# The ninth tap as plain fp32 products on four row groups

## The chip, the cores and the metric

The kernel runs on one core of one Trainium2 chip. The metric is the device time of one execution in microseconds, the median of several runs. The core has five engines with instruction queues of their own: TensorE (PE; its weight loads are shown apart, as PEld), VectorE (DVE), ScalarE (ACT), GpSimd (POOL) and SyncE (SP), which here only issues transfers.

## The reference

The input x has 4 images of 16 channels, 256 x 256, fp32. There are two layers, each a residual block on a group norm (`_gn`, 8 groups). The change touches only the first:

```python
def _L0_conv_ref(x, conv_w, conv_b):
    out = conv_general_dilated(x, conv_w, (1, 1), 'SAME') + conv_b    # 16 -> 16*25 channels, 3 x 3
    logits = out.reshape(N, C, K * K, H, W)                           # K = 5
    weights = softmax(logits, axis=2)                                 # over the 25 places
    return einsum('ncuij,ncuij->ncij', _unfold(x), weights)           # weighted mean of a 5 x 5 window

x = x + _L0_conv_ref(_gn(x), conv_w, conv_b)
x = x + _L1_conv_ref(_gn(x), ...)                                     # splines and SiLU, then 3 x 3
```

With h = `_gn(x)`, every pixel and channel gets 25 logits from a 3 x 3 convolution of h. A softmax over them weighs the 5 x 5 window of h around the pixel.

## The kernel before

**Where the data lie.** h is written to device memory in two layouts. `hs` holds rows of h, by strips of 32 columns, for the windows (`u`). `hst` holds h transposed, one column of 128 rows after another, for the convolution. A third array `hsl` holds h transposed in two parts: `hi`, h rounded to the type fp32r, and `lo`, the rest h - `hi`, also in fp32r.

**Getting h.** `normalize` (L276 on) is a generator; each `yield` is a place where the main loop goes on with its own work. `rows` has ScalarE scale x into `hsp` (L346) and `ht` (L359). `columns` transposes four blocks of `ht` on TensorE into `tp` (L384), copies `tp` to `tt` (fp32) and to `hi` (L375 to L381, `hi` always on ScalarE), and has VectorE subtract to `lo` (L396). Small copies carry the border rows of each half (L329, L330, L377 to L381, L405). `put_columns` then issues three writes, `tt` to `hst` and `hi` and `lo` to `hsl` (L319). Half of image 0 is normalized before layer 0 begins (`part=0`), among the statistics of x; the other half and images 1 to 3 go on inside layer 0, one image ahead. So while the last image is worked on, nothing of this remains.

**Layer 0.** The loop runs over 64 strips (4 images, 2 halves of 128 rows, 8 strips of 32 columns). The 128 rows of a half are the partitions of the result. A strip has eight steps of four columns (`JG = 4`). One column is a convolution of 128 pixels: 9 taps x 16 channels = 144 rows of weights, and a bias. 128 of them fit into one product: `am` holds eight taps of h (8 x 16 partitions) for eight columns, and `wm` their weights, both fp32 (L878). The ninth tap and the bias go into a second product (L882) with 97 rows in fp32r: `an` holds `hi` and `lo` twice each and a row pair of ones, `wn` the weights, rounded and rest, so that the products of the halves add up to about fp32. Each fp32 product stands in the profile as two weight loads and two passes, each fp32r product as one of each.

A column's 400 logits lie in one bank of `lg`, two columns to a tile, three such tiles in turn. ScalarE takes two columns at a time out of `lg` with an exponential into `e` (L901), GpSimd multiplies `e` with the window `u` (L906), and VectorE sums both over the 25 places into `nd` (L738), one step later. After eight steps VectorE divides (L758 to L760) with a reciprocal from ScalarE (L752, L754), GpSimd subtracts from x (L766), and every fourth strip ScalarE takes statistics for the next layer's norm (L786).

`e` has four buffers, `am` and `an` three each (`NIM = 3`), `u` two. All loads stand in SyncE's queue: `am` (three, L686) and `an` (two, L696) for eight columns, asked for two blocks ahead, and `u` (five, L710) for a strip, asked for at the middle of the strip before. The writes of `normalize` are in the same queue. Instructions are in the program's order on each engine (`in_order`).

**Layer 1** follows on the same engines. What matters of it here is that its products (L1082, L1092) use 32 columns of weights, in four column groups, and that L1092 changes between 64 and 128 rows.

**Before layer 0**, `prepare0` builds `wm` and `wn`, and a bound on the logits from the weights (`wps`, `times`) and from x decides whether the softmax needs a shift. It doesn't with these inputs (`shift` is false).

Of the kernel before, what the change touches and what calls it, by code (L numbers as in the profile page):

```python
# [12 lines left out]
F32 = mybir.dt.float32  # L13
F32R = mybir.dt.float32r
# [21 lines left out]
def conv_preact_kernel(  # L36
# [16 lines left out]
    P = 128  # L53
# [34 lines left out]
    hsl = [[dram.tile([C, 2, CT], F32, name=f"hsl{b}_{h}") for h in range(NH)] for b in range(B)]  # L88

# [27 lines left out]
    KT = 6 * C + 1  # L117
    wn = const.tile([KT, K, C, K], F32R, name="wn")

# [103 lines left out]
    NIM = 3  # L223

    def norm_tiles(prep):


        xps = [prep.tile([P, QC, W + 2 * PAD], F32, name=f"xp{h}", bufs=1) for h in range(NH)]
        tts, his, los = [
            [prep.tile([P, NH, QG, RP], d, name=f"{v}{n}", bufs=1) for n in range(2)]  # L230
            for v, d in (("tt", F32), ("hi", F32R), ("lo", F32R))
        ]
# [3 lines left out]
        for t in (*tts, *his, *los):  # L236
            t = t if t.dtype == F32 else t.bitcast(F32)
            nc.gpsimd.memset(t[:, 0, :, 0:1], 0.0)
            nc.gpsimd.memset(t[:, NH - 1, :, RP - 1 :], 0.0)
        return prep, xps, tts, his, los  # L240
# [7 lines left out]
    def zeros(b, queue):  # L248

        for e in (0, HP - PAD):  # L250
            for r in range(PAD):
                yield partial(
                    queue.dma_start,
                    hs[b][:, e + r].rearrange("s c w -> c s w"),
                    zero[0:C, 0 : NST * SP].rearrange("c (s w) -> c s w", s=NST),
                )
        for h in range(NH):
            for w in (0, (W + 1) * RP):
                yield partial(queue.dma_start, hst[b][h][:, w : w + RP], zero[0:C, 0:RP])
                yield partial(  # L260
                    queue.dma_start,
                    hsl[b][h][:, :, w : w + RP].rearrange("c t r -> (c t) r"), zero[:, 0:RP],
                )
# [4 lines left out]
    kept = [  # L268
        const.tile([P, C // QC * NQ, QG, 1], d, name=f"kept{i}") for i, d in enumerate((F32, F32R, F32R))
    ]  # L270

    def normalize(b, ptr, tiles, held=None, copier=None, part=None, dense=False):
# [5 lines left out]
        prep, xps, tts, his, los = tiles  # L278
# [32 lines left out]
        def put_columns(q, n):  # L311
            g0 = n * QG
            for h in parts:

                for to, ti, t in ((hst, 0, tts[n]), (hsl, 0, his[n]), (hsl, 1, los[n])):
                    d = to[b][h]
                    m = 2 if to is hsl else 1
                    t = t if t.dtype == F32 else t.bitcast(F32)
                    nc.sync.dma_start(  # L319
                        bass.AP(  # L320
                            tensor=d.tensor,
                            offset=d.offset + q * QC * m * CT + ti * CT + (1 + g0) * RP,
                            ap=[[QW * RP, W // QW], [m * CT, QC], [1, QG * RP]],
                        ),
                        t[:, h].rearrange("p g r -> p (g r)"),
                    )

        def border(t):
            nc.scalar.copy(t[:, 1, :, 0:1], t[:, 0, :, P : P + 1])  # L329
            nc.scalar.copy(t[:, 0, :, RP - 1 :], t[:, 1, :, 1:2])  # L330
# [37 lines left out]
        def columns(q, n, h):  # L368
# [3 lines left out]
            def copy(t, to, keep):  # L372

                if h in parts:
                    to(t[:, h, :, 1 : 1 + P], tp)  # L375
                if part == 1:
                    to(t[:, 1, :, 0:1], keep[:, q * NQ + n])  # L377
                elif h == 1:
                    to(t[:, 0, :, RP - 1 :], tp[:, :, 0:1])
                else:  # L380
                    to(t[:, 1, :, 0:1] if part is None else keep[:, q * NQ + n], tp[:, :, P - 1 :])  # L381

# [6 lines left out]
            copy(tts[n], copier, kept[0])  # L389
            copy(his[n], nc.scalar.copy, kept[1])  # L390
            if not dense:
                yield

            v = slice(1, 1 + P) if h in parts else slice(RP - 1, RP)
            to = h if h in parts else 0
            nc.vector.tensor_sub(  # L396
                los[n][:, to, :, v], tp[:, :, 0 : v.stop - v.start],
                his[n][:, to, :, v].bitcast(F32),
            )
            if part == 0 and h == 0:  # L400
                moves.append((1, partial(
                    nc.scalar.copy, kept[2][:, q * NQ + n], los[n][:, 0, :, P : P + 1]
                )))
            if part == 1:
                nc.scalar.copy(los[n][:, 1, :, 0:1], kept[2][:, q * NQ + n])  # L405
            if h == NH - 1:
                if part is None:
                    moves.append((5, partial(border, los[n])))
                moves.append((9 if part is None else 4, partial(put_columns, q, n)))
# [32 lines left out]
    with tc.tile_pool(name="prep0", bufs=2) as prep, tc.tile_pool(  # L442
# [29 lines left out]
        wnr = pre.tile([KT, NL], F32, name="wnr")  # L472
        nc.vector.memset(wnr, 0.0)
        v = conv_wt[2, 2 * C : 3 * C]
        for r in (0, 2 * C):
            nc.sync.dma_start(
                wnr[r : r + 2 * C, :],
                bass.AP(tensor=v.tensor, offset=v.offset, ap=[v.ap[0], [0, 2], [1, NL]]),
            )
        for r in (4 * C, 6 * C):  # L480
            nc.sync.dma_start(wnr[r : r + 1, :], conv_b)
# [24 lines left out]
        def prepare0():  # L506
# [3 lines left out]

            wp = pre.tile([KT, K, C, K], F32, name="wp")
            for m in range(K):
                nc.gpsimd.tensor_copy(wm[:, m], places(wr)[:, m])
                nc.gpsimd.tensor_copy(wp[:, m], places(wnr)[:, m])
            whi = pre.tile([KT, K, C, K], F32R, name="whi")
            nc.scalar.copy(whi, wp)
            nc.vector.tensor_sub(wn, wp, whi.bitcast(F32))
            nc.scalar.copy(wn[0 : 2 * C], wp[0 : 2 * C])
            nc.scalar.copy(wn[4 * C : 4 * C + 1], wp[4 * C : 4 * C + 1])

            aw = pre.tile([P, 2, NL], F32, name="aw")
            nc.scalar.activation(aw[:, 0], wr, AF.Square)
            nc.scalar.activation(aw[0:KT, 1], wnr, AF.Square)
            times = pre.tile([KT, 1], F32, name="times")
            nc.vector.memset(times, 0.0)
            nc.vector.memset(times[0 : 4 * C], 0.25)
            nc.vector.memset(times[4 * C : 4 * C + 1], 1.0)  # L530
            nc.tensor.matmul(wps, lhsT=onec, rhs=aw[:, 0], start=True, stop=False)
            nc.tensor.matmul(wps, lhsT=times, rhs=aw[0:KT, 1], start=False, stop=True)
# [125 lines left out]
    def layer0(shift):  # L658
# [4 lines left out]
        with tc.tile_pool(name=f"prep{arm}", bufs=2) as prep, tc.tile_pool(  # L663
# [6 lines left out]
            ans = [imp.tile([KT, CI * RP], F32R, name=f"an{n}{arm}", bufs=1) for n in range(NIM)]  # L670
            for t in ans:

                nc.vector.memset(t.bitcast(F32)[4 * C : KT], 1.0)
# [4 lines left out]
            def load_im(n):  # L678
# [14 lines left out]
                an = ans[n % NIM]  # L693
                d = hsl[b][hf]
                for r in (0, 2 * C):
# [7 lines left out]
                return am, an  # L703

            def load_u(n):
                b, hf, s = strips[n]
                u = l0.tile([P, K, C, SP], F32, name=f"u_{n}{arm}", tag="u")
# [125 lines left out]
            ims.append(load_im(1))  # L833
            nxc, xc = load_xc(0), None
            ahead = iter(())
            for n, (b, hf, s) in enumerate(strips):
# [23 lines left out]
                for j in range(0, SW, JG):  # L860
                    if j % CI == 0:
                        k = n * nci + j // CI
                        if k + 2 < len(strips) * nci:
                            ims.append(load_im(k + 2))
                        am, an = ims.pop(0)
# [7 lines left out]
                    e = l0.tile([P, 2, JG, K, C, K], F32, name=f"e_{n}_{j}{arm}", tag="e", bufs=LAG + 3)  # L873
                    for j1 in range(0, JG, 2):
                        lg = plog.tile([P, 2, 512], F32, name=f"lg_{n}_{j}_{j1}{arm}", tag="lg")
                        for i in range(2):
                            o = (j + j1 + i) % CI * RP
                            nc.tensor.matmul(  # L878
                                lg[:, i, :NL], lhsT=am[:, o : o + P],
                                rhs=wm.rearrange("p m c d -> p (m c d)"), start=True, stop=False,  # L880
                            )
                            nc.tensor.matmul(  # L882
                                lg[:, i, :NL], lhsT=an[:, o : o + P],
                                rhs=wn.rearrange("p m c d -> p (m c d)"), start=False, stop=True,
                            )
# [321 lines left out]
```

## Time and profile before

| | us |
|---|---|
| median of 3 runs | 3048.94 (3048.42 to 3060.75) |
| span of the profiled execution | 3050.8 |
| first to last L878 product of layer 0 (start) | 113.8 to 2022.8 |
| busy in that stretch of 1909 us: PE, DVE, ACT, POOL | 1823, 1882, 1206, 1857 |
| share of the DMA engines in that stretch | 0.80 |
| DMA bytes over the span | 628 MB |

Busy times count when an instruction of the engine was under way. The ends of matmuls are modelled, and consecutive ones overlap in their pipeline, so what TensorE needs is read from the distance of the starts and not from busy time. "Idle before" is how long an engine stood still ahead of the instructions of a group, and "<-" what released it.

### The profile page before, as it was taken

To read this page: it belongs to the slowest core of one execution; us is meant where nothing else is said; L and a number is where in the kernel's file an instruction comes from. 1 tells how busy PE (TensorE), PEld (TensorE's weight loads), DVE (VectorE), ACT (ScalarE), POOL (GpSimd) and SP (SyncE) were. 2 spreads that over 40 slices of the span, in tenths; PEclk is the share of its full clock that TensorE was granted. 3 is DMA by queue.
4 is the path that set the end of the run, shared out by engine and by line. 5 is a ranking of instruction groups with operands and counts; after the bars stand their busy time and mean duration, and the time that the engine had idled before them with its cause. 6 is when DMAs were issued, how large, how long until landed. Compare 5 with 4: busy or idle time off the path is not lost.

```text
span 3050.8 us, 39867 instructions
## 1 busy us (share of the span) xinstructions
PE 2804.2 (92%) x14280; PEld 1447.6 (47%) x14280; DVE 2954.8 (97%) x1587; ACT 2252.1 (74%) x2619; POOL 1948.5 (64%) x744
## 2 busy tenths in 40 slices
PE   4699999999989999999999999958999999999998
PEld 3465656656656666666666556632222222222222
DVE  7599999999999999999999999999999999999997
ACT  6566776576765666766645646559999999999996
POOL 4399999999999999999999999980100100000000
PEclk7799999999999999999999999979999999999999
DMA  8988988878978778878857667659999999999993
GB/s 274 254 232 223 261 238 238 230 196 247 244 207 229 201 207 226 241 209 228 234 152 194 179 165 191 162 128 208 201 192 195 195 195 190 199 195 199 192 199 86
DMA packets 353042, 628.40 MB, mean 206 GB/s; under 512 B 41394, under 2 KB 218788, under 8 KB 336964
## 3 DMA queue, kind: packets, MB, share of 16 engines
q1 hardware_dynamic: 320132, 607.39, 81.0%
q10 hardware_dynamic: 30960, 15.73, 1.7%
q8 instruction: 117, 1.92, 0.3%
q0 software_dynamic: 1744, 2.64, 0.3%
q14 instruction: 89, 0.73, 0.1%
HBM read 516.05 MB, written 104.24 MB: 203 GB/s over the span
## 4 chain that ended last, share of the span: by engine, by line
DVE 68%; issue 12%; PE 9%; DMA 5%; ACT 3%; POOL 2%; SPq 1%; DVEq 0%; POOLq 0%; ACTq 0%
DVE nd L738 43%; PE lg L878 6%; DVE ta L169 4%; DVE ta L168 4%; DVE tb L169 4%; DVE tb L168 4%; DVE tb L159 2%; PE lg L882 2%; DVE yo L1065 1%; POOL e L906 1%; DVE r L759 1%; DMA an<-hsl 1%; DVE nd L758 1%; DVE nd L760 1%; DVE lo L396 1%
## 5 line engine op out<-in xcount | busy, mean ns | idle before, releaser
L906 POOL TENSOR_TENSOR e<-e,u 128x1600 f32<-128x1600 f32 x512 | 1788.5, 3543 | 56.4 <-ACT e L901 49.0
L878 PE MATMUL lg<-wm,am 128*128 128x400 f32 x4096 | 1735.7, 505 | 80.3 <-ACT e L901 49.1
L738 DVE TENSOR_REDUCE nd<-e 128x128 f32<-128x3200 f32 x512 | 1749.2, 3478 | 24.3 <-POOL e L906 24.3
L882 PE MATMUL lg<-wn,an 97*128 97x400 f32 x2048 | 1344.3, 656 | 12.8 <-DMA an<-hsl 12.7
L901 ACT ACTIVATE e<-lg 128x800 f32<-128x800 f32 x1024 | 820.0, 837 | 682.8 <-DVE nd L738 440.7
L878 PEld LDWEIGHTS lg<-wm,am 128*128 128x128 f32 x4096 | 759.9, 192 | 400.1 <-ACT e L901 104.5
L1082 PE MATMUL yp<-ring,wt 128*32 128x512 f32 x6144 | 745.3, 597 | 86.6 <-DVE ring L170 62.6
L882 PEld LDWEIGHTS lg<-wn,an 97*128 97x128 f32 x2048 | 388.1, 190 | 330.7 <-issue 21.7
L1082 PEld LDWEIGHTS yp<-ring,wt 128*32 128x32 f32 x6144 | 202.2, 109 | 621.6 <-issue 433.1
L999 POOL MEMSET sl<- 16x256 f32 x6 | 1.8, 306 | 402.9 <-PE yp L1092 396.8
L169 DVE TENSOR_TENSOR ta<-ta,ta 128x2048 f32<-128x2048 f32 (+1 forms) x64 | 147.4, 2303 | 3.0 <-ACT ta L167 2.9
L170 DVE SCALAR_TENSOR_TENSOR ring<-ta,ta 128x2048 f32<-128x2048 f32 (+1 forms) x64 | 147.8, 2310 | 2.5
L786 ACT ACTIVATE z<-xc,nrm 128x256 f32<-128x256 f32 x240 | 144.2, 601 | 6.4 <-POOL xc L766 2.4
L170 DVE SCALAR_TENSOR_TENSOR ring<-tb,tb 128x2048 f32<-128x2048 f32 x64 | 145.6, 2275 | 2.5
L169 DVE TENSOR_TENSOR tb<-tb,tb 128x2048 f32<-128x2048 f32 x64 | 145.2, 2269 | 0.0
L1092 PE MATMUL yp<-sl,ws 64*32 64x512 f32 (+1 forms) x1032 | 131.2, 602 | 0.0
L999 POOL MEMSET slc<- 16x256 f32 x2 | 0.6, 309 | 203.1 <-PE yp L1092 203.0
L167 ACT ACTIVATE ta<-ta 128x2048 f32<-128x2048 f32 (+1 forms) x64 | 123.4, 1928 | 2.0
L194 POOL TENSOR_TENSOR d<-d,nrz 128x8 f32<-128x8 f32 x4 | 2.7, 680 | 189.9 <-DVE d L192 189.9
L167 ACT ACTIVATE tb<-tb 128x2048 f32<-128x2048 f32 x64 | 120.6, 1884 | 0.0
L1018 ACT ACTIVATE sl<-sl,q 64x2048 f32<-64x2048 f32 x43 | 90.0, 2094 | 1.2
L766 POOL TENSOR_TENSOR xc<-xc,nd 128x512 f32<-128x512 f32 x64 | 82.8, 1293 | 8.3 <-DVE nd L760 8.3
(200 smaller groups left out, 2108.8 us busy)
## 6 DMA issues: line engine op xcount, KB each, us to landing
am<-hst SPq DMA_DIRECT2D x512, 194.6 KB
u<-hs SPq DMA_DIRECT2D x320, 288.0 KB
an<-hsl SPq DMA_DIRECT2D x512, 129.8 KB
xta<-x1s SPq DMA_DIRECT2D x40, 1024.0 KB
xtb<-x1s SPq DMA_DIRECT2D x40, 1024.0 KB
xtc<-x1s SPq DMA_DIRECT2D x40, 1024.0 KB
am<-hst SPq DMA_DIRECT2D x256, 129.8 KB
sl<-x1s SPq DMA_DIRECT2D x166, 128.0 KB
```

The source lines that it names most:

```text
L167: nc.scalar.activation(s1, r1, AF.Square, scale=2.0)
L168: nc.vector.scalar_tensor_tensor(s2, t, 2.0, s2, ALU.subtract, ALU.mult)
L169: nc.vector.tensor_mul(s1, s1, r1)
L170: nc.vector.scalar_tensor_tensor(f, s2, 0.0, s1, ALU.min, ALU.subtract if given else ALU.add)
L738: nc.vector.tensor_reduce(nd[:, :, :, j : j + JG].rearrange("p t c j -> p t j c"), e.rearrange("p t j m c d -> p t j c m d"), AX.XY, ALU.add,)
L786: nc.scalar.activation(z, v, f, scale=nrm[b][:, 0, g : g + 1], bias=nrm[b][:, 1, g : g + 1], accum_out=st1[b][:, t, g, columns_of(n) : col ...
L878: nc.tensor.matmul(lg[:, i, :NL], lhsT=am[:, o : o + P], rhs=wm.rearrange("p m c d -> p (m c d)"), start=True, stop=False,)
L882: nc.tensor.matmul(lg[:, i, :NL], lhsT=an[:, o : o + P], rhs=wn.rearrange("p m c d -> p (m c d)"), start=False, stop=True,)
L901: nc.scalar.activation(ev, lg[:, :, :NL], AF.Exp)
L906: nc.gpsimd.tensor_tensor(e[:, 1].rearrange("p j m c d -> p j (m c) d"), e[:, 0].rearrange("p j m c d -> p j (m c) d"), uv, ALU.mult,)
L1082: nc.tensor.matmul(yp[t * M : (t + 1) * M], lhsT=wt[:, d, e].rearrange("p r o -> p (r o)"), rhs=ring[:, r0 + t * RT + d : r0 + t * RT + d ...
L1092: nc.tensor.matmul(yp[t * M : (t + 1) * M], lhsT=ws[v, e].rearrange("p r o -> p (r o)"), rhs=sl[n % 3][v, t : t + NT + 1 : NT, e : e + W], ...
```

## The change

The ninth tap and the bias become one plain fp32 product of 17 rows (16 channels and a row of ones). Four columns are put on the partitions 0, 32, 64 and 96 of one tile, `wn` is there four times, and the four products of a step stand behind its eight-tap products, each on 32 rows of the array. `hi`, `lo`, `hsl` and everything that made and moved them go. The new tile `ans` holds a whole strip: row group r has the columns r, r+4, r+8 and so on, loaded by four transfers from `hst`, inside `load_u`. `am` gets a fourth buffer and is asked for three blocks ahead, `u` gets a third.

```diff
-    KT = 6 * C + 1
-    wn = const.tile([KT, K, C, K], F32R, name="wn")
+    KT = C + 1
+    RG = 32
+    wn = const.tile([P, K, C, K], F32, name="wn")
...
-    NIM = 3
+    NIM = 4
...
-            copy(tts[n], copier, kept[0])
-            copy(his[n], nc.scalar.copy, kept[1])
+            t, keep = tts[n], kept[:, q * NQ + n]
+            if h in parts:
+                copier(t[:, h, :, 1 : 1 + P], tp)
...
-            nc.vector.tensor_sub(
-                los[n][:, to, :, v], tp[:, :, 0 : v.stop - v.start],
-                his[n][:, to, :, v].bitcast(F32),
-            )
...
-            ans = [imp.tile([KT, CI * RP], F32R, name=f"an{n}{arm}", bufs=1) for n in range(NIM)]
+            ans = [imp.tile([P, SW // JG, P], F32, name=f"an{n}{arm}", bufs=1) for n in range(3)]
...
-                an = ans[n % NIM]
-                d = hsl[b][hf]
-                for r in (0, 2 * C):
+                return am
+
+            def load_u(n):
+                b, hf, s = strips[n]
+                d = hst[b][hf]
+                for r in range(JG):
                     nc.sync.dma_start(
-                        an.bitcast(F32)[r : r + 2 * C, 0:run],
+                        ans[n % 3][r * RG : r * RG + C],
                         bass.AP(
-                            tensor=d.tensor, offset=d.offset + (j0 + 2) * RP + 2,
-                            ap=[[2 * CT, C], [CT, 2], [1, run]],
+                            tensor=d.tensor, offset=d.offset + (s * SW + r + 2) * RP + 2,
+                            ap=[[CT, C], [JG * RP, SW // JG], [1, P]],
                         ),
                     )
-                u = l0.tile([P, K, C, SP], F32, name=f"u_{n}{arm}", tag="u")
+                u = l0.tile([P, K, C, SP], F32, name=f"u_{n}{arm}", tag="u", bufs=3)
...
-            ims.append(load_im(1))
+            ims += [load_im(1), load_im(2)]
...
-                        if k + 2 < len(strips) * nci:
-                            ims.append(load_im(k + 2))
+                        if k + 3 < len(strips) * nci:
+                            ims.append(load_im(k + 3))
...
+                    lgs = [
+                        plog.tile([P, 2, 512], F32, name=f"lg_{n}_{j}_{j1}{arm}", tag="lg")
+                        for j1 in range(0, JG, 2)
+                    ]
+                    for i in range(JG):
+                        o = (j + i) % CI * RP
+                        nc.tensor.matmul(
+                            lgs[i // 2][:, i % 2, :NL], lhsT=am[:, o : o + P],
+                            rhs=wm.rearrange("p m c d -> p (m c d)"), start=True, stop=False,
+                        )
+                    for i in range(JG):
+                        k = slice(i * RG, i * RG + KT)
+                        nc.tensor.matmul(
+                            lgs[i // 2][:, i % 2, :NL], lhsT=ans[n % 3][k, j // JG],
+                            rhs=wn[k].rearrange("p m c d -> p (m c d)"), start=False, stop=True,
+                        )
                     for j1 in range(0, JG, 2):
-                        lg = plog.tile([P, 2, 512], F32, name=f"lg_{n}_{j}_{j1}{arm}", tag="lg")
-                        for i in range(2):
-                            o = (j + j1 + i) % CI * RP
-                            nc.tensor.matmul(
-                                lg[:, i, :NL], lhsT=am[:, o : o + P],
-                                rhs=wm.rearrange("p m c d -> p (m c d)"), start=True, stop=False,
-                            )
-                            nc.tensor.matmul(
-                                lg[:, i, :NL], lhsT=an[:, o : o + P],
-                                rhs=wn.rearrange("p m c d -> p (m c d)"), start=False, stop=True,
-                            )
+                        lg = lgs[j1 // 2]
```

In `put_columns` one write of `tt` is left of three. `prepare0` places `wn` directly and needs no rounded copy and no `times`.

More of the change, by code (lines that the diff above doesn't have):

```diff
@@ L2 @@
 from functools import partial
-from itertools import chain
 from itertools import chain
@@ L86, in conv_preact_kernel @@
     hst = [[dram.tile([C, CT], F32, name=f"hst{b}_{h}") for h in range(NH)] for b in range(B)]
-    hsl = [[dram.tile([C, 2, CT], F32, name=f"hsl{b}_{h}") for h in range(NH)] for b in range(B)]
     CP = H * W + 1024
@@ L222, in conv_preact_kernel @@
     nrz = [const.tile([P, 2, G], F32, name=f"nrz{b}") for b in range(B)]
-    NIM = 3
+    NIM = 4
     def norm_tiles(prep):
         xps = [prep.tile([P, QC, W + 2 * PAD], F32, name=f"xp{h}", bufs=1) for h in range(NH)]
[L229 to L232, printed above, removed]
+        tts = [prep.tile([P, NH, QG, RP], F32, name=f"tt{n}", bufs=1) for n in range(2)]
         for t in xps:
@@ L235, in norm_tiles @@
             nc.gpsimd.memset(t[:, :, PAD + W :], 0.0)
-        for t in (*tts, *his, *los):
-            t = t if t.dtype == F32 else t.bitcast(F32)
+        for t in tts:
             nc.gpsimd.memset(t[:, 0, :, 0:1], 0.0)
             nc.gpsimd.memset(t[:, NH - 1, :, RP - 1 :], 0.0)
-        return prep, xps, tts, his, los
+        return prep, xps, tts
     zero = const.tile([PAD * C, max(RP, NST * SP)], F32, name="zero")
@@ L259, in zeros @@
                 yield partial(queue.dma_start, hst[b][h][:, w : w + RP], zero[0:C, 0:RP])
-                yield partial(
-                    queue.dma_start,
-                    hsl[b][h][:, :, w : w + RP].rearrange("c t r -> (c t) r"), zero[:, 0:RP],
-                )
     NQ = QW // QG
-    kept = [
-        const.tile([P, C // QC * NQ, QG, 1], d, name=f"kept{i}") for i, d in enumerate((F32, F32R, F32R))
-    ]
+    kept = const.tile([P, C // QC * NQ, QG, 1], F32, name="kept")
     def normalize(b, ptr, tiles, held=None, copier=None, part=None, dense=False):
-        prep, xps, tts, his, los = tiles
+        prep, xps, tts = tiles
         copier = copier or nc.scalar.copy
@@ L313, in put_columns @@
             for h in parts:
[L315 to L325, printed above, removed]
-                    )
-        def border(t):
-            nc.scalar.copy(t[:, 1, :, 0:1], t[:, 0, :, P : P + 1])
-            nc.scalar.copy(t[:, 0, :, RP - 1 :], t[:, 1, :, 1:2])
+                d = hst[b][h]
+                nc.sync.dma_start(
+                    bass.AP(
+                        tensor=d.tensor, offset=d.offset + q * QC * CT + (1 + g0) * RP,
+                        ap=[[QW * RP, W // QW], [CT, QC], [1, QG * RP]],
+                    ),
+                    tts[n][:, h].rearrange("p g r -> p (g r)"),
+                )
         hts = {}
@@ L370, in columns @@
             tp = ptr.tile([P, QG, P], F32, name=f"tp{b}_{q}_{n}_{h}", tag="tp")
[L372 to L381, printed above, removed]
             for k in range(QG):
@@ L388, in columns @@
                 yield
-            copy(tts[n], copier, kept[0])
-            copy(his[n], nc.scalar.copy, kept[1])
+            t, keep = tts[n], kept[:, q * NQ + n]
+            if h in parts:
+                copier(t[:, h, :, 1 : 1 + P], tp)
+            if part == 1:
+                copier(t[:, 1, :, 0:1], keep)
+            elif h == 1:
+                copier(t[:, 0, :, RP - 1 :], tp[:, :, 0:1])
+            else:
+                copier(t[:, 1, :, 0:1] if part is None else keep, tp[:, :, P - 1 :])
             if not dense:
                 yield
-            v = slice(1, 1 + P) if h in parts else slice(RP - 1, RP)
-            to = h if h in parts else 0
-            nc.vector.tensor_sub(
-                los[n][:, to, :, v], tp[:, :, 0 : v.stop - v.start],
-                his[n][:, to, :, v].bitcast(F32),
-            )
[L400 to L405, printed above, removed]
             if h == NH - 1:
-                if part is None:
-                    moves.append((5, partial(border, los[n])))
-                moves.append((9 if part is None else 4, partial(put_columns, q, n)))
+                moves.append((5 if part is None else 4, partial(put_columns, q, n)))
             yield
@@ L471, in conv_preact_kernel @@
             )
-        wnr = pre.tile([KT, NL], F32, name="wnr")
+        wnr = pre.tile([P, NL], F32, name="wnr")
         nc.vector.memset(wnr, 0.0)
-        v = conv_wt[2, 2 * C : 3 * C]
-        for r in (0, 2 * C):
[L476 to L481, printed above, removed]
+        for r in range(0, P, RG):
+            nc.sync.dma_start(wnr[r : r + C, :], conv_wt[2, 2 * C : 3 * C])
+            nc.sync.dma_start(wnr[r + C : r + KT, :], conv_b)
         nm = 3 * C
@@ L509, in places @@
                 return t.rearrange("p (c m d) -> p m c d", c=C, m=K)
-            wp = pre.tile([KT, K, C, K], F32, name="wp")
             for m in range(K):
                 nc.gpsimd.tensor_copy(wm[:, m], places(wr)[:, m])
[L514 to L519, printed above, removed]
+                nc.gpsimd.tensor_copy(wn[:, m], places(wnr)[:, m])
             aw = pre.tile([P, 2, NL], F32, name="aw")
             nc.scalar.activation(aw[:, 0], wr, AF.Square)
[L526 to L530, printed above, removed]
+            nc.scalar.activation(aw[0:KT, 1], wnr[0:KT], AF.Square)
             nc.tensor.matmul(wps, lhsT=onec, rhs=aw[:, 0], start=True, stop=False)
-            nc.tensor.matmul(wps, lhsT=times, rhs=aw[0:KT, 1], start=False, stop=True)
+            nc.tensor.matmul(wps, lhsT=onec[0:KT], rhs=aw[0:KT, 1], start=False, stop=True)
         def prepare1():
@@ L669, in layer0 @@
         ) as plog, tc.tile_pool(name=f"prc{arm}", bufs=1, space=PSUM) as prc:
-            ans = [imp.tile([KT, CI * RP], F32R, name=f"an{n}{arm}", bufs=1) for n in range(NIM)]
+            ans = [imp.tile([P, SW // JG, P], F32, name=f"an{n}{arm}", bufs=1) for n in range(3)]
             for t in ans:
-                nc.vector.memset(t.bitcast(F32)[4 * C : KT], 1.0)
+                nc.vector.memset(t, 1.0)
             tiles = norm_tiles(prep)
@@ L692, in load_im @@
                     )
-                an = ans[n % NIM]
-                d = hsl[b][hf]
-                for r in (0, 2 * C):
+                return am
[3 more added lines that the diff above has]
+                for r in range(JG):
                     nc.sync.dma_start(
-                        an.bitcast(F32)[r : r + 2 * C, 0:run],
+                        ans[n % 3][r * RG : r * RG + C],
                         bass.AP(
-                            tensor=d.tensor, offset=d.offset + (j0 + 2) * RP + 2,
-                            ap=[[2 * CT, C], [CT, 2], [1, run]],
-                        ),
-                    )
-                return am, an
-            def load_u(n):
-                b, hf, s = strips[n]
-                u = l0.tile([P, K, C, SP], F32, name=f"u_{n}{arm}", tag="u")
+                            tensor=d.tensor, offset=d.offset + (s * SW + r + 2) * RP + 2,
+                            ap=[[CT, C], [JG * RP, SW // JG], [1, P]],
+                        ),
+                    )
+                u = l0.tile([P, K, C, SP], F32, name=f"u_{n}{arm}", tag="u", bufs=3)
                 for m in range(K):
@@ L862, in layer0 @@
                         k = n * nci + j // CI
-                        if k + 2 < len(strips) * nci:
-                            ims.append(load_im(k + 2))
-                        am, an = ims.pop(0)
+                        if k + 3 < len(strips) * nci:
+                            ims.append(load_im(k + 3))
+                        am = ims.pop(0)
                     if j == SW // 2:
@@ L873, in layer0 @@
                     e = l0.tile([P, 2, JG, K, C, K], F32, name=f"e_{n}_{j}{arm}", tag="e", bufs=LAG + 3)
[L874 to L885 removed]
+                    lgs = [
[13 more added lines that the diff above has]
+                            rhs=wn[k].rearrange("p m c d -> p (m c d)"), start=False, stop=True,
+                        )
+                    for j1 in range(0, JG, 2):
+                        lg = lgs[j1 // 2]
                         ev = e[:, 0, j1 : j1 + 2].rearrange("p j m c d -> p j (m c d)")
```

## The prediction

> **What bounds the kernel now.** I first read the granted clock (0.975 over the whole span, 0.99 between 113.8 and 2022.8 us, so the clock is no issue), then the busy times in stretches, then the groups of layer 0, then single stretches of the timeline. Layer 1 is not touched by the change; layer 0 runs from the first `lg` product at 113.8 us to the last one at 2022.8 us. The groups of the window from 113 to 2040 us (busy time, mean ns of one, idle time before them):
>
> ```profile
> L906 POOL TENSOR_TENSOR e<-e,u 128x1600 f32<-128x1600 f32 x512 | 1788.5, 3543 | 56.4 <-ACT e L901 49.0 <-DMA u<-hs 3.9 <-DMA an<-hsl 3.4
> L738 DVE TENSOR_REDUCE nd<-e 128x128 f32<-128x3200 f32 x512 | 1749.2, 3478 | 24.3 <-POOL e L906 24.3
> L901 ACT ACTIVATE e<-lg 128x800 f32<-128x800 f32 x1024 | 820.0, 837 | 682.8 <-DVE nd L738 440.7 <-PE lg L882 220.0 <-DMA u<-hs 8.2
> L396 DVE TENSOR_TENSOR lo<-tp,hi 128x512 fp32r<-128x512 f32 x56 | 38.1, 681 | 0.0
> L384 PE MATMUL tp<-ident,ht 128*128 128x128 f32 x224 | 34.1, 274 | 0.0
> ```
>
> The reader sees three engines close together. A strip of 32 columns is eight steps of four columns. VectorE paces it, as the last image shows:
>
> ```profile
> 1500.58 27.23 DVE L738 TENSOR_REDUCE nd<-e 128x128 f32<-128x3200 f32 x8
> 1527.73 0.68 DVE L758 TENSOR_TENSOR nd<-nd,r 128x512 f32<-128x512 f32 x1
> 1528.44 0.70 DVE L759 SCALAR_TENSOR_TENSOR r<-nd,r 128x512 f32<-128x512 f32 x1
> 1529.17 0.69 DVE L760 TENSOR_TENSOR nd<-nd,r 128x512 f32<-128x512 f32 x1
> 1529.78 27.23 DVE L738 TENSOR_REDUCE nd<-e 128x128 f32<-128x3200 f32 x8
> ```
>
> From 1500.58 to 1529.78 is 29.2 us with no gap. In images 0 to 2 each `lo` of L396 lengthens a strip by 0.6 us, to 29.8 or 30.4. GpSimd needs 8 x 3.49 (1788.5 / 512) + 1.29 (L766) = 29.2 us per strip as well: no edit of the change touches that, so **29.2 us per strip is a floor**. TensorE starts a column every 0.855 us (0.338 from the first pass of L878 to its second, 0.026 to the record of L882, 0.49 to the next column), 3.42 us per step, 27.4 us per strip, plus 0.6 us per group of four transposes. Its reserve is only 29.2 - 27.4 = 1.8 us per strip, **0.22 us per step**.
>
> **The products, part by part.** Today a column has two passes of `wm` and one L882 pass. The stream of one fp32 pass of 400 columns is about 0.335 us; the L882 pass takes 0.855 - 2 x 0.34 = 0.175 us, 0.70 us for four columns. New: 8 `wm` passes of 0.34 = 2.72 us, then four columns on four row groups, two passes each, 0.335 us per pass. If the four groups run abreast that is 2 x 0.335 + 0.02 = 0.69 us: the same as today. The trace has no row groups, but column groups of fp32 in layer 1, at 0.112 us for a 512-column instruction (10.51 / 94) against a stream of 0.335 x 512/400 = 0.43 us, so 3.8 abreast:
>
> ```profile
> 3015.34 10.51 PE yp L1082 x94
> ...
> 3025.84 2.98 PE yp L1092 x24
> ```
>
> What is new is that TensorE changes its shape twice a step, from whole array to quarter rows and back. Two rows price it. The first is L207, a 16-row product between two columns of layer 0, where nothing else changes:
>
> ```profile
> 1778.38 0.83 PE L878 MATMUL lg<-wm,am 128*128 128x400 f32 x2
> 1778.74 0.65 PE L882 MATMUL lg<-wn,an 97*128 97x400 f32 x1
> 1779.32 0.38 PE L207 MATMUL ps<-q,sel 16*128 16x2 f32 x2
> 1779.63 0.94 PE L878 MATMUL lg<-wm,am 128*128 128x400 f32 x2
> ```
>
> The next column would have come at 1778.38 + 0.855 = 1779.23; L207 starts only at 1779.32, 0.09 after the stream before it has ended, and its weights are loaded then and not ahead. Afterwards the `wm` pair takes 0.94 instead of 0.83 to 0.84: its weight load of 128 columns stands exposed for 0.10. So one change costs 0.09 + 0.10, about 0.20 us. The second row is L1092, where 64-row and 128-row products of 32 columns alternate (weight loads, eight in each shape):
>
> ```profile
> 2068.28 0.15 PEld L1092 LDWEIGHTS yp<-sl,ws 64*32 64x32 f32 x8 [0.84 <-issue]
> 2069.27 0.16 PEld L1092 LDWEIGHTS yp<-sl,ws 128*32 128x32 f32 x8 [0.84 <-issue]
> 2070.27 0.15 PEld L1092 LDWEIGHTS yp<-sl,ws 64*32 64x32 f32 x8 [0.84 <-issue]
> ```
>
> Two rounds of 0.43 are 0.86, the spacing is 1.00: 0.14 us per change. I take 0.20, from L207, because it has the 128 columns of weights and lies in this very stage; 0.14 stays as the lower bound, and for the upper see the third case below. A step is then 2.72 + 0.69 + 2 x 0.20 = **3.81 us** (3.69 with 0.14), against 3.65 for VectorE and GpSimd. TensorE becomes the bound.
>
> A rule of the Trainium skill speaks against the change: "TensorEngine Tiling (Array Packing)", Key Properties, says that a change of tiling mode drains the array, which the gap before L207 agrees with; it gives no time. The same skill, "TensorE: Matmul & The Clock Gate", Measured speedup vs the span model, has 3.07 times for four row tiles; by it the four columns would take 4 x 0.67 / 3.07 = 0.87 us, an estimate, and a step 3.99 us.
>
> **The layer.** 512 x 3.81 = 1951, plus 56 transpose groups x 0.6 = 34, plus waits. Of today's 1909 us, 512 x 3.42 + 34 = 1785 are work and 124 are waits. Most of these are VectorE's pace handed back through `e` and `lg` (PE and PEld waiting for ACT e L901, 49 and 104 us overlapping) and vanish when TensorE is slower; I keep 15, what its waits for `am` cost now (16.3). Sum 2000, **+91 us**.
>
> **What is removed, and what it is worth.** L396 (38.1 us in layer 0) leaves VectorE: worth 38 us only while VectorE is the bound, nothing under a TensorE step of 3.81. ScalarE loses the `hi` copies (56 x 0.616 = 34.5) and the small `hi` and `lo` copies (96 x 0.22 + 16 x 0.22 = 24): it idles 682.8 us before L901, so nothing. The loads of `an` (512 x 129.8 KB = 66 MB) become 256 loads of 64 KB (17 MB), two of three writes of L319 go (33 MB): 83 MB less of some 409 MB; DMA at 0.80 is not what strips wait for, apart from the 12 us of `an` waits inside the 124. SyncE issues 4 x 0.99 us per strip for `an` now and some 4 x 0.46 later; its own waits for L882 are 531 us, so nothing. The fourth `am` removes at most the 16 us named, the third `u` at most the 12 us of waits at the start.
>
> **Before layer 0** ScalarE is busy without a gap from 60 to 80 us, and the chain there passes through `hi` and `lo` pieces of 0.5 to 0.8 us. I take 4 us off (0 to 9, the latter being all `hi` and kept copies there). The start of layer 0 gives 3 us (first strip 36.7 us against 29.2; two `an` blocks fewer in the queue, but the four new loads of 0.46 stand ahead of the first `u`, and a third `am` ahead of `xc`; bounds -6 to +2).
>
> **The new order.** All eight `wm` passes come first, so both `lg` of a step are ready together; with three `lg`, the next step's second pair needs the first one back after 2 x 0.68 + 0.20 = 1.56 us. The exponential takes 0.84 and some 0.15 to be seen, if ScalarE is free: a reserve of about 0.5 us, where it was about 2.4 (two `lg` of 1.71 less 1.0). Statistics (L786, two of 0.79 per step) and `ht` (1.3) can overrun it; queued behind such a wait is PE's whole stream. Bounds 0 to 56 steps x 0.8 = 45 us; I take nothing, since 3.81 - 1.68 leaves ScalarE 2.1 us a step for some 0.8 us of other work on average.
>
> **Sum**: 3050.8 (span) + 91 - 4 - 3 = 3135; the median of the runs is 1.9 us below the span, so **3133 us**. Its own range: 3075 (switch 0.14: 512 x 0.12 = 61 less) to 3190 (45 us of `lg` waits and 15 more).
>
> **Rivals.**
> 1. *The switches hide.* If a change of shape costs 0.08 or less, a step is at most 2.72 + 0.69 + 0.17 = 3.58, a strip 8 x 3.58 + 0.6 = 29.2, and the floor of VectorE and GpSimd decides. Then L396's 38 us come off: 3048.9 - 38 - 7 = 3004. For it: the loads of one row group could slip behind another's stream, and L1082's loads do. Against: L207's loads did not. 22%.
> 2. *Between*: changes of 0.09 to 0.13, within 0.5% of before, about 3050. 8%.
> 3. *The four weight loads of 128 columns queue.* L207's two loads start 0.107 apart; three more in line are 0.32 a step, step 4.13: 512 x 0.32 = 164 more, 3297. 15%.
> 4. *The row groups do not run abreast.* In program order a column's two passes stand together; if passes start strictly in order, the four columns take five rounds, 1.68 us, step 4.80, 3640 us; one after another, 2.70, some 4160 us. The skill's clock-gate page (What overlaps and what doesn't) says products start in strict order, which would make it 3640; L1082, whose passes do start four at a time, is against. 8%.
>
> My forecast, TensorE bound at 3.7 to 3.9 us a step, has 47%.
>
> **How the numbers follow.** Half a per cent, 15 us, is what a measurement here can tell. Faster is rival 1 (0.22), no change is rival 2 (0.08), the rest is slower (0.70). Range 2998 to 3300: it leaves out rival 4 and the edges of rivals 1 and 3; the likeliest alone 3075 to 3190.
>
> **What would show it.** Right: strips of about 30.5 us in the last image, VectorE idle before L738 with waits for GpSimd and ScalarE, ScalarE waiting for PE and no longer for `nd`, a gap of some 0.2 us at each change of shape, four starts within 0.03 us. Wrong if the last image's strips stay at 29.2 (rival 1), if starts in the group lie 0.1 apart (rival 3), or 0.3 (rival 4). A step near 3.6 with large PE waits for ScalarE would mean that the order of the eight passes, not the change of shape, costs.

## The result and the profile after

The changed kernel takes 3103.61 us (median of four runs, 3097.74 to 3106.01) against 3049.76 us: a ratio of 1.0166, 95% interval 1.0147 to 1.0184, so it is slower by 54 us. Its profiled execution has a span of 3101.5 us at a granted clock of 0.98, 50.7 us above the span of before. In the timelines the first `lg` product starts at 108.98 us instead of 113.78, the last at 2072.64 instead of 2022.84. Layer 0 thus grew from 1909.1 to 1963.7 us (+54.6), what lies ahead of it shrank by 4.8, and what follows takes 1028.9 instead of 1028.0.

The page of the kernel after: the chain that ended last, by engine, and four groups (busy time, mean ns of one, idle time before them and what ended it).

```profile
PE 59%; DVE 20%; issue 9%; POOL 4%; DMA 4%; ACT 3%; SPq 1%; DVEq 0%; POOLq 0%; ACTq 0%
...
L851 POOL TENSOR_TENSOR e<-e,u 128x1600 f32<-128x1600 f32 x512 | 1795.9, 3522 | 100.5 <-ACT e L846 92.6
L677 DVE TENSOR_REDUCE nd<-e 128x128 f32<-128x3200 f32 x512 | 1757.2, 3481 | 95.6 <-POOL e L851 95.5
...
L846 ACT ACTIVATE e<-lg 128x800 f32<-128x800 f32 x1024 | 801.8, 835 | 798.1 <-PE lg L825 795.5
```

L677 is the sum that was L738, L851 the multiplication that was L906, L846 the exponential that was L901; L819 and L825 are now the eight-tap and the ninth-tap product. ScalarE waited for VectorE (`nd`) before; now nearly all of its 798 us are a wait for TensorE, and VectorE and GpSimd each stand idle for some 100 us. In two stretches of layer 0 (length, then busy us and records of each engine, granted clock, DMA share, GB/s) TensorE has no idle time left at full clock:

```profile
core 0: us, PE busy (x) PEld busy (x) DVE busy (x) ACT busy (x) POOL busy (x), PEclk, DMA share, GB/s
900.00:1200.00 300.00, 300.00 (x1295) 140.92 (x1294) 288.47 (x110) 184.45 (x314) 288.12 (x90) 1.00 0.66 173
1500.00:1800.00 300.00, 300.00 (x1278) 139.52 (x1280) 288.26 (x123) 165.25 (x277) 291.08 (x100) 1.00 0.58 151
```

One step in the timeline (start, duration, engine and line):

```profile
1902.65 2.31 PEld L819 LDWEIGHTS lg<-wm,am 128*128 128x128 f32 x8 [0.57 <-issue]
1902.65 2.95 PE L819 MATMUL lg<-wm,am 128*128 128x400 f32 x8
...
1905.54 0.31 PEld L825 LDWEIGHTS lg<-wn,an 17*128 17x128 f32 x8 [0.57 <-issue]
1905.54 0.95 PE L825 MATMUL lg<-wn,an 17*128 17x400 f32 x8
...
1906.42 2.31 PEld L819 LDWEIGHTS lg<-wm,am 128*128 128x128 f32 x8 [0.57 <-issue]
1906.42 2.95 PE L819 MATMUL lg<-wm,am 128*128 128x400 f32 x8
```

From one group of eight `wm` passes to the next are 1906.42 - 1902.65 = 3.77 us; the median over layer 0 is 3.768. The single records behind these lines: passes of one shape start 0.336 us apart. From the last `wm` pass to the first of the quarter rows it is 0.429 (0.093 more), and the first pass in a new shape takes 0.440 (0.104 more), because its weights, whose load otherwise starts with the pass before, load only when that pass itself is due (both records of L825 start at 1905.54); that is the "0.57 <-issue" in front of both loads. The four products of the group start at 1905.538, .545, .551 and .558, their second passes from 1905.978 on: the row groups do run abreast. So a step is ten rounds of 0.336 = 3.36 plus 0.41 for **two changes of shape at 0.205 us each** (the 0.02 of the stagger is in it).

### The profile page after: what moved, and what is told of

Read it like the earlier page. It is cut to its first block, busy times and chain, and to the rows that moved or that the text cites. A ratio compares the mean times of both kernels' runs of the same rounds, so it can differ in the third digit from the quotient of the medians.

```text
span 3101.5 us, 42625 instructions
## 1 busy us (share of the span) xinstructions
PE 2941.8 (95%) x16328; PEld 1198.7 (39%) x16328; DVE 2928.1 (94%) x1511; ACT 2197.0 (71%) x2416; POOL 1960.8 (63%) x724
## 4 chain that ended last, share of the span: by engine, by line
PE 59%; DVE 20%; issue 9%; POOL 4%; DMA 4%; ACT 3%; SPq 1%; DVEq 0%; POOLq 0%; ACTq 0%
PE lg L819 43%; PE lg L825 13%; DVE ta L167 4%; DVE ta L166 4%; DVE tb L167 4%; DVE tb L166 4%; POOL e L851 3%; DVE tb L157 2%; DVE yo L1010 1%; PE tp L352 1%; DMA slc<-x1s 1%; PE yp L1027 1%; DMA xin<-in_x_dram 1%; DVE ring L168 1%; DMA xta<-x1s 1%
## 5 line engine op out<-in xcount | busy, mean ns | idle before, releaser
L851 POOL TENSOR_TENSOR e<-e,u 128x1600 f32<-128x1600 f32 x512 | 1795.9, 3522 | 100.5 <-ACT e L846 92.6
L677 DVE TENSOR_REDUCE nd<-e 128x128 f32<-128x3200 f32 x512 | 1757.2, 3481 | 95.6 <-POOL e L851 95.5
L819 PE MATMUL lg<-wm,am 128*128 128x400 f32 x4096 | 1512.9, 512 | 13.2 <-DMA an<-hst 8.5
L846 ACT ACTIVATE e<-lg 128x800 f32<-128x800 f32 x1024 | 801.8, 835 | 798.1 <-PE lg L825 795.5
L819 PEld LDWEIGHTS lg<-wm,am 128*128 128x128 f32 x4096 | 738.2, 190 | 723.4 <-issue 243.0
L825 PE MATMUL lg<-wn,an 17*128 17x400 f32 x4096 | 489.2, 547 | 0.0
L825 PEld LDWEIGHTS lg<-wn,an 17*128 17x128 f32 x4096 | 160.1, 183 | 293.3 <-issue 286.4
```

What stands on the lines that cost most here:

```text
L677: nc.vector.tensor_reduce(nd[:, :, :, j : j + JG].rearrange("p t c j -> p t j c"), e.rearrange("p t j m c d -> p t j c m d"), AX.XY, ALU.add,)
L819: nc.tensor.matmul(lgs[i // 2][:, i % 2, :NL], lhsT=am[:, o : o + P], rhs=wm.rearrange("p m c d -> p (m c d)"), start=True, stop=False,)
L825: nc.tensor.matmul(lgs[i // 2][:, i % 2, :NL], lhsT=ans[n % 3][k, j // JG], rhs=wn[k].rearrange("p m c d -> p (m c d)"), start=False, stop ...
L846: nc.scalar.activation(ev, lg[:, :, :NL], AF.Exp)
L851: nc.gpsimd.tensor_tensor(e[:, 1].rearrange("p j m c d -> p j (m c) d"), e[:, 0].rearrange("p j m c d -> p j (m c) d"), uv, ALU.mult,)
```

## The experiments

The theory to be tested: the changes of shape alone made TensorE the bound; neither the order of the products, nor the number of passes as such, nor the loads decide. Ratios are to the kernel before, on the same chip; the edits are shown in short.

**The new order alone.** The kernel before, with the eight-tap products of four columns first and then four fp32r ninth products over 97 rows; no change of shape.

```diff
-   for i in range(2): product of wm, then product of wn, into lg
+   for i in range(JG): product of wm into lgs[i // 2]
+   for i in range(JG): product of wn (97 rows, fp32r) into lgs[i // 2]
```

> The kernel before, with its fp32r products, but in the new order: the eight-tap products of the four columns first, then the four ninth-tap products, so that both lg of a step are ready together; no change of shape. Theory (each change of shape costs 0.2 us and TensorE becomes the bound): TensorE still starts a step every 3.42 us, VectorE stays the bound, 3040 to 3060 us. Rival (the order costs, because the reserve until the first lg is needed again falls from 2.4 to 0.5 us): 3085 us or more, with TensorE waiting for ScalarE's exponentials.

Measured: 3057.69 us, ratio 1.0021 (1.0004 to 1.0037). The order and both `lg` coming ready together cost at most 0.4%.

**The changes of shape taken away.** The kernel after, with the ninth tap as one fp32r pass per column over all 128 rows, the weights of the three other row groups being zero.

```diff
-   wn[k], ans[n % 3][k, j // JG]          (17 rows, fp32: two passes)
+   wn[:, i], ans[n % 3][:, j // JG]       (128 rows, fp32r: one pass)
```

> The changed kernel, with the ninth tap and bias as one fp32r pass over all 128 rows (the weights of the other three groups are zero) instead of fp32 on row groups; loads, buffers and order as in the changed kernel. The terms of the rounding of h and of the weights of the ninth tap are left out. Theory: no change of shape, step 3.42 us on TensorE, so VectorE and GpSimd pace the strips at 29.2 us and the 38 us of lo are gained: 2995 to 3015 us. Rival (order or loads cost): 3060 us or more.

Measured: 3019.83 us, ratio 0.9896 (0.9878 to 0.9915), some 5 us above what was expected, and faster than both kernels. The page of this run:

```profile
DVE 81%; issue 9%; DMA 2%; POOL 2%; PE 2%; ACT 2%; SPq 1%; DVEq 0%; POOLq 0%; ACTq 0%
...
L681 DVE TENSOR_REDUCE nd<-e 128x128 f32<-128x3200 f32 x512 | 1745.2, 3479 | 22.8 <-POOL e L854 22.6
...
L849 ACT ACTIVATE e<-lg 128x800 f32<-128x800 f32 x1024 | 801.7, 835 | 700.8 <-DVE nd L681 368.9
```

The chain has gone from TensorE back to VectorE, and ScalarE waits for `nd` again. The edit also swaps the products: eight passes abreast, two rounds or 0.67 us, become four in a row. But these take 3.41 - 8 x 0.336 = 0.72 us (3.41 is the usual distance of two steps here), so the time of the products hardly changed; what went is the 0.41 of the changes. The next two runs change the one without the other.

**One more change of shape.** The kernel after, with a two-column product over 17 rows of zeros in the middle of the `wm` passes.

```diff
+   if i == 2: nc.tensor.matmul(lgs[0][:, 0, 0:2], lhsT=ans[n % 3][0:KT, j // JG],
+                               rhs=zero[0:KT, 0:2], start=False, stop=False)
```

> The changed kernel with a product of 17 rows and 2 columns of zeros in the middle of the eight-tap products, so that TensorE changes its shape four times a step instead of twice; the result stays the same. Theory: the detour costs what L207's did, 0.5 us a step, all of it on the bound: 512 x 0.5 = 256 us, 3330 to 3380 us. Rival (the 17-row products cost, not the change): two passes of two columns, below 0.1 us a step, 3105 to 3160 us.

Measured: 3349.42 us (one execution), span 3347.5, that is 246 us above after, 0.48 us a step, for a product of two columns. Its timeline (L824 is the `wm` product, L820 the inserted one, L830 the ninth tap):

```profile
1902.92 1.61 PE L824 MATMUL lg<-wm,am 128*128 128x400 f32 x4
...
1904.46 0.38 PE L820 MATMUL lg<-zero,an 17*128 17x2 f32 x2
...
1904.77 1.61 PE L824 MATMUL lg<-wm,am 128*128 128x400 f32 x4
...
1906.31 0.95 PE L830 MATMUL lg<-wn,an 17*128 17x400 f32 x8
```

Four passes, 1.34 us, lead from one change to the next, yet 1904.46 - 1902.92 and 1906.31 - 1904.77 are 1.54: each run of four passes carries 0.20, the exposed load at its start and the gap at its end, which is one change of shape.

**Both changes kept, one round of passes less.** The kernel after, its 17-row products in fp32r.

```diff
-   wn = const.tile([P, K, C, K], F32, name="wn")
+   wn = const.tile([P, K, C, K], F32R, name="wn")
-   ans = [imp.tile([P, SW // JG, P], F32, ...
+   ans = [imp.tile([P, SW // JG, P], F32R, ...
```

> The kernel after with the same 17-row products on four row groups, but in one fp32r pass instead of two fp32 passes (the rests of the rounding are left out); two changes of shape a step stay, one pass of the group (0.336 us) becomes one of about half a pass and the other goes. Theory (the changes cost 0.205 us each, but a sum under VectorE's 3.65 costs nothing): TensorE 8 x 0.336 + 0.41 + 0.18 to 0.35 = 3.28 to 3.45 us a step, VectorE's 3.65 decides: 3000 to 3030 us. Rival (each change of shape puts a wait into the chain whatever TensorE's sum is): 3070 to 3105 as the kernel after.

Measured: 3016.39 us, ratio 0.9888 (0.9871 to 0.9904), the fastest of all. The two changes are still there (from the last `wm` pass to the group 0.429 us, the first `wm` pass 0.440, as in after), and an undisturbed step of TensorE is 3.27 us, 0.50 less than in after; only steps behind a transpose group are shorter, 3.17. The chain that ended last is VectorE's:

```profile
DVE 79%; issue 9%; DMA 3%; POOL 2%; ACT 2%; PE 2%; SPq 1%; DVEq 0%; POOLq 0%; ACTq 0%
...
L846 ACT ACTIVATE e<-lg 128x800 f32<-128x800 f32 x1024 | 801.6, 835 | 704.3 <-DVE nd L677 524.3
```

So a change of shape does no harm of itself; it costs 0.205 us of TensorE, and that counts only when TensorE's sum passes that of the next engine. In these runs a sum of 3.41 us a step costs nothing and one of 3.77 does; VectorE's 3.65 lies between.

**The floor.** The kernel after without the four products of the ninth tap.

> The kernel after with the four products of the ninth tap and the bias left out (the output lacks that tap and the bias); their loads, buffers and everything else stay. Theory (VectorE with 3.65 us a step is the next bound once TensorE is under it; the third u and fourth am buffer and the shorter start change little): TensorE has eight passes of 0.336, 2.69 us a step, no change of shape; VectorE's 3.65 decides, so 512 x 3.65 plus what the run with the whole-array fp32r product left over: 3000 to 3025 us, no faster than that run's 3020 by over 0.7%. Rival (TensorE's share still decides a part, or the waits of the after kernel come from its loads): under 2950, or over 3060.

Measured: 3020.39 us, ratio 0.9909 (0.9893 to 0.9926). TensorE's least step falls to 2.69 us, and nothing is gained on the two runs before: 2.69, 3.27 and 3.41 us of TensorE give 3020, 3016 and 3020 us. All three keep the loads, the buffers and the order of after, so none of these made it slow. In these three runs layer 0 takes 1872 to 1874 us from the first `lg` product to the last, 35 to 37 us less than before. VectorE's busy time in that stretch is 1849 to 1850 us against 1882.5, 33 us less, and its idle time 2 to 4 us less: this fits the subtraction of L396 (38.1 us of records, which overlap their neighbours a little), which the change had taken from VectorE, though no run puts L396 back alone.

**Half as many changes.** If the changes are the cost, turning the order about in every other step (eight, ninth, ninth, eight) should halve it. This needs four `lg` tiles, which fill PSUM; the transposes therefore use one of them, and `r` moved to SBUF.

```diff
+   for f, first in zip((ninth, eight) if j // JG % 2 else (eight, ninth), (True, False)): f(first)
-   r = prc.tile([P, C, SW], F32, ...)              (PSUM)
+   r = l0.tile([P, C, SW], F32, ..., bufs=1)       (SBUF)
```

> The changed kernel, with the order turned about in every other step (ninth-tap products first, then eight-tap products), so that two groups of row-group products stand next to each other and TensorE changes its shape once per step on the mean, half as often. For that lg has four buffers, the transposes take one of them, and the reciprocal r lies in SBUF. Theory: 3.77 - 0.2 = 3.57 us a step, 28.5 us a strip and some 0.5 for transposes, so the floor of 29.2 us holds again: 3000 to 3030 us. Rival (the row-group products themselves are slow): no gain, 3090 us or more. Rival (lg reserve): between, TensorE waiting for ScalarE.

Measured: 3444.01 us, ratio 1.1290 (1.1259 to 1.1321): a miss by over 400 us. In its timeline the second ninth-tap group starts two columns at a time, waiting for ScalarE to give back an `lg`, and after such waits the `wm` passes run 0.667 us apart instead of 0.336 (L836 is the ninth tap, L828 the `wm` product, L860 the exponential):

```profile
1903.33 0.30 PEld L836 LDWEIGHTS lg<-wn,an 17*128 17x128 f32 x4 [1.59 <-ACT e L860]
...
1904.06 0.30 PEld L836 LDWEIGHTS lg<-wn,an 17*128 17x128 f32 x4 [0.43 <-ACT e L860]
...
1905.18 7.04 PE L828 MATMUL lg<-wm,am 128*128 128x400 f32 x16
```

I took the waits inside the group for the cause and moved them away:

```diff
+   if odd:  eight(True); held = new_lgs(next step)
+            for t in held: two-column product of zeros (whole array) into t
+            ninth(False)
+   else:    ninth(True); eight(False)
```

> The order turned about in every other step once more (half as many changes of shape), but with what spoiled it taken away: the two logit tiles of the second step are written (two columns of zeros, whole array) ahead of the first step's ninth group, so that a wait for ScalarE falls between whole-array products and not between the two groups; transposes and their copies only come after a pair and in one go, and the scales' tile is given back at once. Theory (the changes of shape decide, and the turned order failed because its second group waited inside): a pair of steps takes 16 x 0.336 + 2 x 0.69 + 0.41 less 0.02 plus some 0.15 for the touches = 7.3 us, 3.65 a step, level with VectorE: 3010 to 3060 us at a clock near 0.98. Rival 1 (two groups in a row, 1.4 us of 17-row products, lower the clock by themselves): over 3250 us at a clock under 0.95. Rival 2 (the waits for free logit tiles stay whatever their place, since four tiles are two steps deep and no more): 3100 to 3400 us, with ScalarE's e waited for in front of the touches.

Measured: 3435.44 us, ratio 1.1265 (1.1246 to 1.1284): a miss too. The time and the lowered clock (0.934) are those of the first rival, and the waits inside the group were not it; but the lines view (groups, 1000 to 1900 us) names something that no theory had:

```profile
L705 DVE TENSOR_TENSOR nd<-nd,r 128x512 f32<-128x512 f32 x26 | 101.1, 3888 | 0.9
L704 DVE SCALAR_TENSOR_TENSOR r<-nd,r 128x512 f32<-128x512 f32 x26 | 94.8, 3645 | 0.9
```

These two operations on `r` take 0.69 us each in the kernel after (its L699 and L698), with `r` in PSUM:

```profile
L698 DVE SCALAR_TENSOR_TENSOR r<-nd,r 128x512 f32<-128x512 f32 x30 | 20.9, 695 | 1.0
L699 DVE TENSOR_TENSOR nd<-nd,r 128x512 f32<-128x512 f32 x30 | 20.6, 686 | 1.0
```

Some 6.2 us more a strip, 64 strips: 400 us. So the next run moved `r` and nothing else.

**`r` in SBUF alone.** The kernel after, with that one line.

> The kernel after with one thing moved: r (the reciprocal, 128x512) lies in SBUF instead of PSUM, as it did in both runs with the turned order. Theory (the turned order lost its time here and not on TensorE: in those traces VectorE's two operations on r took 3.65 and 3.89 us instead of 0.69 each, while GpSimd multiplied in SBUF; TensorE's stops and its passes of 0.667 us follow from that): a strip on VectorE is 8 x 3.65 = 29.2 plus 6.2 to 6.6 us = 35.6, against TensorE's 30.1, so 64 x 5.5 = 350 us more than after: 3420 to 3480 us, with the two operations at 3 to 4 us in the lines view and TensorE's changes as many as before. Rival (the order of the products and the four logit tiles were what cost it): 3095 to 3130, as after.

Measured: 3490.32 us, ratio 1.1449 (1.1428 to 1.1470), 10 us above the expected range: the order is as in after, and the loss is there. The expectation counted two operations on `r`; the third, L697, stretches too, on the mean from 0.68 to 2.05 us. VectorE's busy time in layer 0 rises by 447 us over after's and its idle time falls by 70, which together are the 377 us that layer 0 grew. The clock is lowered here as well (0.940), without two groups in a row: so that sign does not speak for the first rival of the run before. The timeline shows how the loss comes about (VectorE's L697 to L699, GpSimd's L851):

```profile
1550.15 3.52 POOL L851 TENSOR_TENSOR e<-e,u 128x1600 f32<-128x1600 f32 x1
...
1551.88 2.34 DVE L697 TENSOR_TENSOR nd<-nd,r 128x512 f32<-128x512 f32 x1
...
1553.84 3.76 POOL L851 TENSOR_TENSOR e<-e,u 128x1600 f32<-128x1600 f32 x1 [0.17 <-ACT e L846]
1554.26 3.89 DVE L698 SCALAR_TENSOR_TENSOR r<-nd,r 128x512 f32<-128x512 f32 x1
...
1558.02 3.51 POOL L851 TENSOR_TENSOR e<-e,u 128x1600 f32<-128x1600 f32 x1 [0.43 <-ACT e L846]
...
1558.18 3.90 DVE L699 TENSOR_TENSOR nd<-nd,r 128x512 f32<-128x512 f32 x1
```

Each of VectorE's records ends 0.55 us after the multiplication of GpSimd that was running: 1551.88 + 2.34 = 1554.22 against 1553.67, 1558.15 against 1557.60, 1562.08 against 1561.53; in the whole run it is 0.55 for all 163 of these records that took over 1.2 us. VectorE, with both inputs in SBUF, does not finish before GpSimd is done. The Trainium skill, "GPSIMD Engine Reference", Specifications, says that GpSimd shares its SBUF interfaces with VectorE and contends with VectorE's instructions of two SBUF inputs; the run agrees, and gives the price: up to 3.2 us an operation here.

**The turned order with `r` in PSUM.** As before, but `r` takes one of the four `lg` tiles for a while.

```diff
+   r = plog.tile([P, 2, 512], F32, ..., tag="lg")[:, 0]     (after an odd step)
```

> The turned order with the early touch as in the run before, but r back in PSUM (it takes one of the four logit tiles for a step and a half in each strip). Half as many changes of shape as after. Theory (r in SBUF was the whole loss): TensorE 7.3 us for a pair of steps, 3.65 a step, VectorE 3.65: 3010 to 3070 us, the two operations on r at 0.7 us, clock 0.96 or more. Rival (two groups in a row or four logit tiles cost by themselves): over 3200.

Measured: 3577.18 us, ratio 1.1728 (1.1708 to 1.1748): a miss again. The operations on `r` are back at 0.69 us, but now the `lg` tile that `r` holds is missing once in each strip (L859 is the product of zeros that opens an `lg`, L847 the ninth tap, L710 the last operation on `r`):

```profile
1719.33 1.63 PE L847 MATMUL lg<-wn,an 17*128 17x400 f32 x16
...
1726.57 1.63 PE L847 MATMUL lg<-wn,an 17*128 17x400 f32 x16
...
1739.34 0.37 PE L859 MATMUL lg<-zeror 128*128 128x2 f32 x1 [5.57 <-DVE nd L710]
...
1739.65 3.05 PE L847 MATMUL lg<-wn,an 17*128 17x400 f32 x16
```

From 1719.33 to 1726.57 is a pair of steps that nothing disturbs: 7.24 us, 3.62 a step, as the theory had it (7.3), and below VectorE's 3.65. Of 255 pairs 97 are like it, at the full clock with two groups in a row, and 25 more only have a transpose group besides. In 63 others, one a strip, TensorE waits for `r`, mostly 5 to 5.6 us, and then runs at half speed (granted clock 0.50 from 1737.0 to 1747.2 us): the group at 1739.65 takes 3.05 us instead of 1.63. The remaining 70 are longer too, without such a wait. Whether half as many changes would bring the whole kernel to 3020 us **stays open**: no run had the turned order and enough PSUM at once. Nor were the fourth `am` and the third `u` buffer tried alone.

## Why the prediction was right, step by step

- **The mechanism was right**: TensorE changes its shape twice a step, at 0.20 us a change, and becomes the bound. Measured 0.205. The size was not quite: 84 us more were forecast, 54 came. The row that priced it, L207 between two columns of the same layer, was the right one; the lower bound of 0.14 from layer 1 holds for 32 columns of weights.
- **The step** was forecast at 3.81 and is 3.768: a pass takes 0.336, not 0.34, eight times, and the group of the quarter rows is two rounds of 0.336, its stagger lying in the 0.41 of the changes. 512 x 0.042 = 21 us less than forecast.
- **The transposes** were given 0.60 us for each of 56 groups, their row in a stream of one shape. Standing after a ninth-tap group they add 0.49 to one step (4.26 us) and take 0.10 from the next (3.67), net 0.39: 12 us less. The transposes meet the change back to the whole array in place of the next `wm` pass, which then starts without an exposed load; this was not thought of.
- **Waits**: 15 forecast; 1963.7 - 512 x 3.768 - 56 x 0.39 = 13. The three add up to the 36 us between the 91 forecast and the 54.6 by which layer 0 grew; all three erred the same way. With 3 us taken off for the start the forecast span was 33 us too long (3135 against 3101.5). The medians lie 29 apart, 3133 against 3104, since the median after came out 2 us above the profiled span and not 1.9 below.
- **L396's 38 us** were held to be worth nothing under a TensorE-bound step, and were: VectorE's idle time before its sums rose from 24.3 to 95.6 us. The three runs with TensorE under 3.65 us brought 35 to 37 us.
- **ScalarE's reserve** of 0.5 us for giving back an `lg` was enough: TensorE's waits for L846 are under 13 us, and the order alone cost 0.2%.
- **Rival 1** (switches hide, 3004 us) had the right floor: 3016 to 3020 was measured where TensorE falls under it. Rival 2 falls with a change at 0.205, rivals 3 and 4 with the starts 7 ns apart. The prediction read the skill's rule that products start in strict order ("TensorE: Matmul & The Clock Gate", What overlaps and what doesn't) so that a column's second pass would hold up the next column's first. The trace has all four first passes ahead of all second ones, so this reading is wrong; whether the rule is, the trace can't tell, as it doesn't hold the order in which the passes were issued. By the same page's 3.07 times for four row tiles (Measured speedup vs the span model) the estimate of a step was 3.99 us, against 3.768: counted alone eight passes take two rounds of 0.336, 4.0 times, but from the group's first start to the next `wm` pass it is 0.88 us, 3.0 times. The estimate added the changes to a figure that may hold them already.
- **The signs named** came: strips of the last image mostly 30.1 to 30.5 us, ScalarE waiting for TensorE, the four starts within 0.02 us.

## What to carry to other kernels

Before splitting the array, count the changes of shape in a steady step, price one from a place in the trace where a small product stands between large ones, and compare the sum with the next engine, not with the engine's own time before: here 0.41 us of changes turned a reserve of 0.22 us into a deficit of 0.12, and dropping one pass of the small products (fp32r, where its rounding can be borne) gave the reserve back, and with it 35 us, about what the change had taken off VectorE. A tile moved out of PSUM to make room can cost more than the room brings, when VectorE reads it together with another SBUF input while GpSimd works.

## What was not expected of the hardware

- VectorE's operation with two inputs in SBUF stretched from 0.69 to 3.89 us beside a GpSimd multiplication, and ended 0.55 us after it each time; with one input in PSUM it kept to 0.69 us, though in the kernel after 152 of the 192 operations on `r` fell within a multiplication of GpSimd.
- After a stop TensorE runs at half speed for a while. In the turned order with early touches, between 1500 and 1800 us, nine stops of 2.6 to 5.5 us (from the start of the last pass to that of the next) were each followed by three to six passes of 0.667 us. In the run without the ninth tap 25 of 46 stops of 2.5 to 3 us between 500 and 1900 us were followed by such passes, none of 36 between 1 and 2 us, and 5 of 199 between 0.7 and 1 us. An engine with reserve thus loses part of it again through its own idle time; in that run this did no harm, as VectorE still set the pace.
